# ReLU moved from POOL to ACT and DVE, and state products added in pairs before the fold, in a scan-attention-FFN kernel

## Chip, core and metric

One core of one Trainium2 chip. The metric is the device time of one execution in microseconds (us), lower is better. PE is TensorE, DVE is VectorE, ACT is ScalarE, POOL is GpSimd. The kernel is already tuned: the work of its engines is interleaved by hand, in a fixed program order.

## The reference, cut to what matters

```python
# x: (4, 64, 64, 96); one layer norm without weights is _ln_t
x = x + conv(_gn(x))                    # group norm, then the scan below
t = tokens(x)                           # (4, 4096, 96)
t = t + linear_attention(_ln_t(t))
t = t + ffn(_ln_t(t))

# conv: proj = layernorm(x) @ W_in: value u, gate g, delta d, and A, B, C with 16 states a channel
def step(h, ins):
    A_t, B_t, C_t, d_t, u_t, g_t = ins
    h_new = d * (A_t * h) + d * (B_t * u_t)
    y = g_t * sum(C_t * h_new, axis=states)
# ... then y @ W_out

# ffn: q_mul rounds to fp8 (e5m2), q_acc to fp16
h = relu(q_acc(q_acc(q_mul(x) @ q_mul(W1).T) + q_mul(b1)))      # 384 wide
y = q_acc(q_acc(q_mul(h) @ q_mul(W2).T) + q_mul(b2))
```

## The kernel before

The work is cut into 32 chunks (4 images of 8), each of 512 positions. In a chunk the 96 channels and 16 states make 12 tiles of 128 partitions: 3 channel groups (`NCG`) times 4 state groups (`NSH`). One step of the program handles one tile; everything else is hung into the steps by `at(step, fn)`.

```python
while s < K or any(q >= s for q in steps):
    # ...
    tiles[s + 1].a_proj()          # PE: A of the next tile
    tiles[s].c_proj()              # PE: C of this tile
    last.keep()                    # ACT: last column of the state
    tiles[s + 1].b_mul()           # POOL: bu = bu * du
    last = tiles[s]; last.scan()   # DVE: h = scan(A, bu)
    tiles[s + 1].a_mul()           # DVE: A = (A + bias) * d
    last.c_mul()                   # DVE: ch = (C + bias) * h
    call(s)                        # what hangs in this step
    tiles[s + 2].b_proj()          # PE
    tiles[s + 2].b_copy()          # ACT: bu = B + bias
```

The products `ch` of each state group are folded over states by PE into one bank `y_ps`, four times a chunk, three matmuls each time:

```python
def state_sum(b, i, sh):
    # ...
    for cg in range(NCG):
        nc.tensor.matmul(y_ps[g][cg * 32 : (cg + 1) * 32, :], lhsT=fold,
            rhs=tiles.pop(g * NT + NCG * sh + cg).ch,
            start=(sh == 0), stop=(sh == NSH - 1), ...)
```

The tail of the previous chunk and the FFN of the previous image ride in the same steps. In the tail, `gated` (the multiply yg, on DVE) comes once a chunk and serves below as its clock mark; `ln.apply` makes xa on ACT, `gram` transposes it into a bank of the tag "M", and `keep` copies that to `xat` on ACT. (A bank is a piece of PSUM, the memory that the program's matmuls write to; a tag names one or more banks that are used in turn.) The FFN of a chunk:

```python
def transpose():                   # PE, then ACT: xq
    ps = bank("B" if drain else "M", [C, TC], f"xq_ps_{nm}")
    # ... four transposes
    nc.scalar.activation(v["xq"], ps, AF.Copy, saturate=False)
def hidden(m):                     # PE; the tag "M" has two banks
    v["h", m] = bank(("C", "Y", "M")[m] if drain else "M", [P, TC], f"h_ps{m}_{nm}")
    nc.tensor.matmul(v["h", m], lhsT=w1_q[:, m * P : (m + 1) * P], rhs=v["xq"], ...)
def relu(m):                       # ACT rounds to fp16, POOL adds the bias and cuts at 0
    # ... hq is made at m == 0, one buffer
    nc.scalar.copy(h16, v["h", m])
    nc.gpsimd.tensor_scalar(hr, h16, b1_q[:, m : m + 1], 0.0, ALU.add, ALU.max)
def quant(m):                      # ACT: to fp8
    nc.scalar.activation(v["hq"][:, m, :], v["hr", m], AF.Copy, saturate=False)
```

The last image's FFN (`drain`) has no scan beside it and runs after the last tile.

## Time and profile before

| | before |
|---|---|
| time, median of 3 runs | 1533.5 us (1532.3 to 1540.0) |
| the execution that the trace shows | 1539.95 us |
| chunk of image 0 | 36.1 us, with group norm 37.8 us |
| chunk with FFN (images 1 to 3) | 40.0 to 40.1 us, with group norm 41.0 us |
| from the start of the first scan to the start of the last ("scan stage") | 1288.3 us |
| from the start of the last scan to the end ("drain") | 122.6 us |

A chunk is timed from yg to yg. Five longer chunks, 43.4 to 49.3 us, are left out of the rows: the first chunk of images 1 and 2 and the fifth of images 0 to 2. The drain is timed here from the last scan and not from the last yg, because the change moves yg by one step and leaves the scan where it is. Ahead of the first scan lies a start-up (the group norm of image 0, the preparation of the weights).

The costliest groups of instructions of the profile before name the parts that the change touches. The columns are line, engine, operation, output and inputs, count, then busy us and mean ns of one, then the idle time of the engine ahead of them and what ended it:

```profile
L735 POOL TENSOR_SCALAR hr<-h,b_q 128x512 f16<-128x512 f16 x96 | 191.9, 2000 | 17.2 <-ACT h L733 16.1
L601 PE MATMUL y_ps<-ch,fold 128*32 128x512 f32 x768 | 136.4, 605 | 0.0
L741 ACT ACTIVATE hq<-hr 128x512 fp8e5<-128x512 f16 x96 | 60.5, 630 | 144.6 <-POOL hr L735 139.8
```

The ReLU on POOL takes 2.0 us each, and ACT stood idle 139.8 us over the run until one of them ended. The y sums (folds of the products over the states) count as 136.4 us of PE. These are the two targets.

### The profile page before, as it was taken

What the parts mean: (1) busy time and instruction counts of PE and PEld (TensorE: products, weight loads), DVE (VectorE), ACT (ScalarE), POOL (GpSimd) and SP (SyncE); (2) the same over time, 40 slices, a digit from 0 to 9 for tenths busy, and PEclk for the clock granted to TensorE, in tenths of its full rate; (3) what the DMA queues carried; (4) which work ended last, traced back from release to release, by engine and by line L of the source; (5) the groups of instructions that cost most, each with busy time, mean ns of one, the idle gap of its engine ahead of it and who ended that gap; (6) DMA issues with size and microseconds to landing.
All of it is one profiled execution on the core that took longest, in us unless ns stands there. A gap on an engine that the chain in (4) does not pass through costs nothing.

```text
span 1538.2 us, 20844 instructions
## 1 busy us (share of the span) xinstructions
PE 1374.3 (89%) x6513; PEld 916.4 (60%) x6513; DVE 1201.0 (78%) x2271; ACT 644.8 (42%) x1501; POOL 984.3 (64%) x868
## 2 busy tenths in 40 slices
PE   5847999999999999989999999989999999998652
PEld 4715666666666666656666666566666666665531
DVE  1007999988999988879999898979999999998330
ACT  2013334433333444544444545434445454443343
POOL 4134555546554777767775777777777777666587
PEclk9999999999999999999999999999999999999555
DMA  7002222222222222221222222212222212220001
GB/s 182 20 9 64 59 62 63 62 47 50 51 56 51 59 67 63 54 50 48 55 55 54 62 59 56 56 42 55 56 55 56 55 47 56 55 56 6 11 11 31
DMA packets 82210, 80.98 MB, mean 53 GB/s; under 512 B 49900, under 2 KB 50384, under 8 KB 82099
## 3 DMA queue, kind: packets, MB, share of 16 engines
q1 hardware_dynamic: 80080, 77.22, 21.1%
q10 hardware_dynamic: 2018, 2.43, 0.7%
q8 instruction: 51, 0.84, 0.2%
q14 instruction: 61, 0.49, 0.1%
HBM read 8.72 MB, written 6.29 MB: 10 GB/s over the span
## 4 chain that ended last, share of the span: by engine, by line
PE 41%; POOL 14%; issue 12%; DVE 12%; ACT 8%; SPq 6%; DMA 4%; POOLq 0%; ACTq 0%; DVEq 0%
PE Cps L155 9%; PE Bps L155 8%; PE Aps L155 7%; POOL bu L554 6%; POOL hr L735 5%; SPq L487 5%; PE y_ps L601 4%; DVE h L570 4%; DVE ch L588 3%; PE dug_ps L155 3%; PE a_ps L705 2%; PE o_ps L624 2%; ACT z L305 2%; DMA d<-d 2%; ACT xn L305 2%
## 5 line engine op out<-in xcount | busy, mean ns | idle before, releaser
L554 POOL TENSOR_TENSOR bu<-bu,du 128x512 f32<-128x512 f32 x384 | 493.9, 1286 | 429.9 <-ACT bu L551 243.4
L570 DVE TENSOR_TENSOR_SCAN h<-Aps,state,bu 128x512 f32<-128x512 f32 x336 | 427.8, 1273 | 89.9 <-POOL bu L554 89.0
L551 ACT ACTIVATE bu<-Bps,b_bac 128x512 f32<-128x512 f32 x384 | 262.3, 683 | 414.0 <-PE Bps L155 398.6
L563 DVE SCALAR_TENSOR_TENSOR Aps<-Aps,b_bac,d 128x512 f32<-128x512 f32 x384 | 283.1, 737 | 32.6 <-PE Aps L155 32.0
L155 PE MATMUL Bps<-xs,w 128*128 128x512 f32 x768 | 273.0, 437 | 15.3 <-ACT bu L551 15.3
L588 DVE SCALAR_TENSOR_TENSOR ch<-Cps,b_bac,h 128x512 f32<-128x512 f32 x384 | 284.9, 742 | 0.5 <-PE Cps L155 0.4
L155 PE MATMUL Cps<-xs,w 128*128 128x512 f32 x768 | 252.7, 410 | 10.1 <-DVE ch L588 10.0
L155 PE MATMUL Aps<-xs,w 128*128 128x512 f32 x768 | 245.6, 401 | 7.9 <-DVE h L570 7.8
L735 POOL TENSOR_SCALAR hr<-h,b_q 128x512 f16<-128x512 f16 x96 | 191.9, 2000 | 17.2 <-ACT h L733 16.1
L155 PEld LDWEIGHTS Cps<-xs,w 128*128 128x128 f32 x768 | 136.8, 189 | 73.5 <-DVE ch L588 47.3
L155 PEld LDWEIGHTS Bps<-xs,w 128*128 128x128 f32 x768 | 130.9, 192 | 81.2 <-issue 35.9
L155 PEld LDWEIGHTS Aps<-xs,w 128*128 128x128 f32 x768 | 144.0, 190 | 47.2 <-DVE h L570 14.5
L155 PE MATMUL Bps<-xl,w 128*128 128x512 f32 x384 | 152.9, 398 | 0.0
L155 PE MATMUL Aps<-xl,w 128*128 128x512 f32 x384 | 152.5, 397 | 0.0
L155 PE MATMUL Cps<-xl,w 128*128 128x512 f32 x384 | 152.4, 397 | 0.0
L601 PE MATMUL y_ps<-ch,fold 128*32 128x512 f32 x768 | 136.4, 605 | 0.0
L741 ACT ACTIVATE hq<-hr 128x512 fp8e5<-128x512 f16 x96 | 60.5, 630 | 144.6 <-POOL hr L735 139.8
L305 ACT ACTIVATE xa<-x,nmr_a,rstd_a 128x96 f32<-128x96 f32 x128 | 49.4, 457 | 113.7 <-DVE nmr_a L301 113.7
L155 PEld LDWEIGHTS Bps<-xl,w 128*128 128x128 f32 x384 | 73.1, 190 | 17.4
L155 PEld LDWEIGHTS Aps<-xl,w 128*128 128x128 f32 x384 | 72.7, 189 | 18.1
L305 ACT ACTIVATE z<-z,nmr_c,rstd_c 128x96 f32<-128x96 f32 x128 | 49.4, 457 | 80.6 <-DVE nmr_c L301 80.6
L155 PEld LDWEIGHTS Cps<-xl,w 128*128 128x128 f32 x384 | 72.4, 188 | 17.7
(157 smaller groups left out, 1735.7 us busy)
## 6 DMA issues: line engine op xcount, KB each, us to landing
d<-d SPq DMA_DIRECT2D x384, 64.0 KB, 2.0
du<-du SPq DMA_DIRECT2D x384, 64.0 KB, 2.0
xl<-lo SPq DMA_DIRECT2D x64, 128.0 KB, 2.3
x<-in_x_dram SPq DMA_DIRECT2D x32, 192.0 KB, 2.8
out_dram<-o SPq DMA_DIRECT2D x32, 192.0 KB, 2.3
w<-w SPq DMA_DIRECT2D x18, 128.0 KB, 2.3
xs<-lo SPq DMA_DIRECT2D x32, 64.0 KB, 2.0
raw<-in_L_conv_W_in_dram ACTq DMA_DIRECT2D x3, 576.0 KB, 5.4
```

Source lines behind the costliest of these rows:

```text
L155: nc.tensor.matmul(ps, lhsT=wt[:, n], rhs=mv, start=(n == 0), stop=(n == 2))
L305: nc.scalar.activation(dst[:, j, 0:C], src[:, j, :], AF.Identity, bias=nmr[:, j : j + 1], scale=self.r[:, j : j + 1],)
L487: nc.sync.dma_start(t[q * 32 : (q + 1) * 32, :], src[cg * 32 : (cg + 1) * 32, :])
L551: nc.scalar.activation(self.bu, self.b_ps, AF.Identity, bias=self.bias(0))
L554: nc.gpsimd.tensor_tensor(self.bu, self.bu, rep["du4", self.b, self.i, self.cg], ALU.mult)
L563: nc.vector.scalar_tensor_tensor(self.a_ps, self.a_ps, self.bias(1), rep["d4", self.b, self.i, self.cg], ALU.add, ALU.mult,)
L570: nc.vector.tensor_tensor_scan(self.h, self.a_ps, self.bu, 0.0 if self.i == 0 else state[self.sh, self.cg], ALU.mult, ALU.add,)
L588: nc.vector.scalar_tensor_tensor(self.ch, self.c_ps, self.bias(2), self.h, ALU.add, ALU.mult)
L601: nc.tensor.matmul(y_ps[g][cg * 32 : (cg + 1) * 32, :], lhsT=fold, rhs=tiles.pop(g * NT + NCG * sh + cg).ch, start=(sh == 0), stop=(sh == ...
L624: nc.tensor.matmul(ps[:, j, :], lhsT=yg[:, j * P : (j + 1) * P], rhs=w_o, start=True, stop=True)
L735: nc.gpsimd.tensor_scalar(hr, h16, b1_q[:, m : m + 1], 0.0, ALU.add, ALU.max)
L741: nc.scalar.activation(v["hq"][:, m, :], v["hr", m], AF.Copy, saturate=False)
```

## The change

Intent: take the ReLU off POOL, give POOL the additions of the state groups pairwise (1 onto 0, 3 onto 2), and let PE fold two pairs a chunk in place of four groups. To make the pairs fit, the fold and the tail come a step later, and the FFN is shifted.

```diff
-FFN0 = 15
+FFN0 = 14
...
-            self.ch = work.tile(..., bufs=6)
+            self.ch = work.tile(..., bufs=8)
...
+    def pair_sum(k):
+        t = tiles.pop(k).ch
+        s = tiles[k - NCG].ch
+        nc.gpsimd.tensor_tensor(s, s, t, ALU.add)
...
-            h16 = work.tile([P, TC], F16, tag="h16", name=f"h16_{m}_{nm}")
+            h16 = work.tile([P, TC], F16, tag="h16", name=f"h16_{m}_{nm}", bufs=1)
             nc.scalar.copy(h16, v["h", m])
-            hr = work.tile([P, TC], F16, tag="hr", name=f"hr_{m}_{nm}")
-            nc.gpsimd.tensor_scalar(
-                hr, h16, b1_q[:, m : m + 1], 0.0, ALU.add, ALU.max
-            )
+            hr = work.tile([P, TC], F16, tag="hr", name=f"hr_{m}_{nm}", bufs=1)
+            bias = b1_q[:, m : m + 1]
+            if drain:
+                nc.vector.tensor_scalar(hr, h16, bias, 0.0, ALU.add, ALU.max)
+            else:
+                nc.scalar.activation(hr, h16, AF.Relu, bias=bias)
...
-            at(s0 + 6 + m, hidden, m)
-            at(s0 + 7 + m, relu, m)
+            at(s0 + 7 + m - drain, hidden, m)
+            at(s0 + 8 + m - drain, relu, m)
             at(s0 + 8 + m, quant, m)
...
-            for sh in range(NSH):
-                at(s0 + NCG * (sh + 1), state_sum, b, i, sh)
-            at(s0 + NT, tail, b, i, s0 + NT)
+            for sh in range(0, NSH, 2):
+                for cg in range(NCG):
+                    at(s0 + NCG * (sh + 1) + cg + 1, pair_sum, s0 + NCG * (sh + 1) + cg)
+                at(s0 + NCG * (sh + 2) + 1, state_sum, b, i, sh)
+            at(s0 + NT, tail, b, i, s0 + NT + 1)
```

(`stop` of the fold follows the new last group, the attention matrix moves from step 8 to 9 so that it stays behind the tail, and the loop keeps a set of tiles already made.)

More of the change, by code (lines that the diff above doesn't have):

```diff
@@ L586, in c_mul @@
         def c_mul(self):
-            self.ch = work.tile([P, TC], F32, tag="ch", name=f"ch_{self.nm}", bufs=6)
+            self.ch = work.tile([P, TC], F32, tag="ch", name=f"ch_{self.nm}", bufs=8)
             nc.vector.scalar_tensor_tensor(
@@ L603, in state_sum @@
                 rhs=tiles.pop(g * NT + NCG * sh + cg).ch,
-                start=(sh == 0), stop=(sh == NSH - 1),
+                start=(sh == 0), stop=(sh == NSH - 2),
                 tile_position=(0, 32 * cg), skip_group_check=True,
@@ L693, in attn_matrix @@
         for n, fn in enumerate((gram_out, gk, kv, ff, r)):
-            at(s0 + 8 + n, fn)
+            at(s0 + 9 + n, fn)
     def ffn(b, i, s0, drain):
@@ L811, in conv_attn_hybrid_kernel @@
         s = FRONT
+        made = set()
         while s < K or any(q >= s for q in steps):
             for k in (s, s + 1, s + 2):
-                if 0 <= k < K and k not in tiles:
+                if 0 <= k < K and k not in made:
+                    made.add(k)
                     tiles[k] = Tile(k)
```

## The prediction

> **What bounds the kernel now.** I read the page's head first, then the busy time by stretch, then who waits for whom on VectorE in one period, then the timeline around one wait and the waits of the last stretch. The page:
>
> ```profile
> PE 1374.3 (89%) x6513; PEld 916.4 (60%) x6513; DVE 1201.0 (78%) x2271; ACT 644.8 (42%) x1501; POOL 984.3 (64%) x868
> ```
>
> PE looks like the bound. But the run has three stages. A chunk (512 positions, 12 tiles) can be timed by the start of its gating multiply yg on DVE, which comes once a chunk: about 36.1 to 37.8 us apart in image 0, which has no FFN beside it (the longer ones carry the next image's group norm), 40.1 or 41.0 us in images 1 to 3, and after the last yg at 1418.9 us a drain of 119 us. The busy time in one chunk of image 0, one of image 3, and the drain:
>
> ```profile
> core 0: us, PE busy (x) PEld busy (x) DVE busy (x) ACT busy (x) POOL busy (x), PEclk, DMA share, GB/s
> 437.29:473.53 36.24, 35.96 (x175) 24.96 (x174) 35.00 (x66) 14.30 (x37) 19.64 (x18) 1.00 0.23 53
> 1227.80:1267.90 40.10, 39.21 (x193) 25.93 (x193) 36.45 (x69) 19.61 (x50) 28.50 (x26) 1.00 0.22 53
> 1418.93:1538.00 119.07, 57.76 (x283) 39.75 (x282) 29.45 (x131) 43.98 (x85) 88.10 (x69) 0.53 0.06 17
> ```
>
> Lines 2 and 3: PE is "busy" 98%, but DVE too, 35.0 of 36.2 and 36.45 of 40.1, and DVE's ends are measured. Who DVE waited for in the image 3 chunk:
>
> ```profile
> DVE h L570 <- POOL bu L554: 3.2, 4, 1.0
> DVE Aps L563 <- PE Aps L155: 0.4, 1, 0.4
> ```
>
> 36.45 busy + 3.2 + 0.4 = 40.05 of 40.10. So **DVE and its waits are the whole period**; PE costs DVE 0.4. Its four waits are for bu, POOL's product ahead of each scan. In the timeline two last 0.96 us and follow four row scalings on ACT; two (0.66, 0.67) stand where POOL runs hr. The first kind:
>
> ```profile
> 1248.27 0.20 DVE L301 SCALAR_TENSOR_TENSOR nmr_f<-mv_f,rstd_f 128x4 f32<-128x4 f32 x1
> 1248.48 1.28 DVE L570 TENSOR_TENSOR_SCAN h<-Aps,state,bu 128x512 f32<-128x512 f32 x1
> 1248.50 1.54 ACT L305 ACTIVATE xn<-x,nmr_f,rstd_f 128x96 f32<-128x96 f32 x4 [0.76 <-DVE nmr_f L301]
> ...
> 1249.95 0.67 ACT L551 ACTIVATE bu<-Bps,b_bac 128x512 f32<-128x512 f32 x1
> ...
> 1250.70 1.29 POOL L554 TENSOR_TENSOR bu<-bu,du 128x512 f32<-128x512 f32 x1 [2.25 <-ACT bu L551]
> ...
> 1252.02 1.28 DVE L570 TENSOR_TENSOR_SCAN h<-Aps,state,bu 128x512 f32<-128x512 f32 x1 [0.96 <-POOL bu L554]
> ```
>
> ACT takes its work in order, so the B copy waits behind the four scalings: nmr to xn to copy to bu to scan, 3.54 us from scan to scan. A plain step of DVE (scan, A product, C product) is 1.20 + 0.64 + 0.65 = 2.5 us. Where the step has no other DVE work, the rest is idle.
>
> The drain is another thing: POOL is busy 88 of 119 us, and
>
> ```profile
> ACT hq L741 <- POOL hr L735: 44.2, 25, 3.1
> DVE xn L312 <- POOL rstd_f L279: 33.3, 8, 6.4
> ```
>
> everything waits for POOL. Between 1485 and 1514 us the chunks follow each other every 9.37 us: three hr of 2.0, rstd 1.27, yb and o 0.9 each make 9.1.
>
> **What the Trainium skill says.** "Perfetto Trace Analysis", section "Identifying the Most-Contended Engine", says that matmul occupancy is not a good measure and that occupancy is, for the vector engines. The trace agrees: PE 98% at 40.1 us, DVE's account closes. "GPSIMD Engine Reference", section 3.1, gives 4497 ns for an fp32 add of 2048; a quarter, 1124, is my estimate for 512, and the trace's like-shaped product takes 1286. Its section 4.1 calls one-input work on POOL roughly line-rate; here the one-input hr took 2000 ns, longer than the two-input product: the measurement decides. "SBUF — State Buffer", section "Who interferes with whom", says that DVE blocks against POOL only with two SBUF inputs or in a 2-port mode. Scan and the A and C products read one tensor from PSUM, so more POOL work shouldn't lengthen them; in the drain the four xn, SBUF to SBUF, took 1.05 us with POOL idle and 2.05 beside it, which agrees. "ScalarE: Activation LUTs", section "Table sets", says relu is in every set, so no table load comes, and the built program has the same two loads as before.
>
> **The change, part by part.**
>
> Counts. PE loses two of four y sums per chunk, 0.99 us each: 64 x 0.99 = 63 us of PE, none of it on DVE's account but the 0.4. POOL loses 96 x 2.0 = 192 us of hr and gets 6 x 32 = 192 adds at 1.29 = 247. ACT gets 72 relus; from hq (0.63, same size, no bias pointer) and bu against xq (683 against 590 ns, with and without pointer), 0.72 each, 52 us on an engine half idle. DVE gets 24 relus in the drain, unknown; my estimate 0.35 (the four xn, 384 fp32 in 1.05 us, are four instructions).
>
> Chunk with FFN. Gone: 0.66 + 0.67 behind hr, and 0.4 for A (the y sum before it goes): -1.7. Come: the compiled order shows what the diff hides. The tail moves a step later and the FFN a step earlier relative to it, so xa (not xn) now stands ahead of the plain step, and on ACT the copy xq comes **between xa and the B copy**, and the copy xat **between z and the B copy**. Each adds 0.48 (ACT's spacing) to the 3.54: 4.02 - 2.58 = 1.44 of idle in place of 0.96, twice: +1.0. In the three steps with pair sums and little else POOL needs 2 x 1.28 = 2.56 against DVE's 2.5: +0.1 to 0.2. In the other three it has 3.5 to 3.85 per step against 3.3 to 3.9 on DVE, with a lead of 1.4 us from the step before: 0. PE's y sum waits for the last pair, then runs nearly level with DVE: +0.2. Sum -1.7 + 1.4 = -0.3; over 23 chunks -7.
>
> Chunk of image 0. No hr to remove. Before, its only notable wait was 0.8 behind z: xa fell before a step that also had row statistics. Now xa lies before the plain step: +1.0; z with xat: +0.6; pairs +0.1; A -0.2. About +1.4 for three chunks; for the five with group norm PE cost 2.1 of waits, of which some 1.5 go, but POOL's centring (0.9) now shares a step with a pair: about +1. Together +9.
>
> So I take **the scan stage as unmoved: +2**.
>
> Drain. In its first part two FFN chunks pass as three rounds of copy, hr, hq (3.25 us from hr to hr), now about 1.75 on ACT; the attention matrix's chain lies beside them, so I count 6 us saved by the first drain chunk. Then eight chunks. POOL per chunk falls to 3.1 us. ACT, in its compiled order, with hq, h16 and hr of one buffer each: hq; wait for the y2 matmuls 1.1; hq 0.63; copy 0.5; relu on DVE and its signals 0.5; hq 0.6; copy 0.5; relu 0.5; copy 0.5; xq 0.5; y16 0.5; hq 0.6 make 6.4. DVE's own order puts xn and statistics (2.1 to 3.1) between two relus, about +0.8. So 7.2 in place of 9.37: 8 x 2.15 = -17. Drain -23.
>
> Sum: 1533.5 + 2 - 23 = 1512. The scan terms come from waits that I add on paper, and several would be smaller with a larger lead of POOL or ACT; I put the middle at **1510**.
>
> **Rivals.**
> (a) PE is the bound as its 98% say. Then 2 us go from each of 32 chunks, and with the drain the time is near 1533 - 63 - 23 = 1447. For it: the chain of waits gives PE 41%. Against: DVE's account closes without PE.
> (b) DVE's waits for POOL's hr go and nothing comes in their place: 23 x 1.7 + 23 = 62, so 1471. Against: the compiled ACT order above.
> (c) POOL becomes late in the pair steps: 12 steps in which it has more than before; 1 us more per chunk is 32 us, near 1540. For it: each pair stands ahead of the next product. Against: POOL is 71% busy at most, 28.5 of 40 us now, and gets 1.7 more.
>
> **Range and chances.** The drain gives 15 to 30 us almost surely. The scan stage may be anything from -25 (part of b) to +20 (part of c). So 1488 to 1530 holds it 8 times in 10. The 2% lines are 1502.9 and 1564.2: faster 0.31, same 0.65, slower 0.04.
>
> **What would show it.** In the profile after: drain from the last yg near 96 us, its chunks some 7 us apart, with POOL's share halved. Image 3 chunks near 39.8 us with two waits of about 1.4 us before scans, behind xa with xq and z with xat; none behind hr. Image 0 chunks near 37.5 and 38.7. If those are below 36 and the FFN chunks near 38, then PE was the bound and rival (a) or (b) is right; if DVE waits over 5 us per chunk right behind the pair sums, (c). A DVE relu near 0.7, or held by POOL, would cut the drain's gain by 8 us.

## The result, and the profile after

| | before | after |
|---|---|---|
| median of 4 runs, same rounds | 1535.1 us (1532.3 to 1540.0) | 1511.2 us (1507.5 to 1514.6) |
| ratio, 95% interval | | 0.984 (0.9805 to 0.9876) |

Ratios in this document are the mean time of one kernel's fast runs over the mean of the other's fast runs of the same rounds, so they are not quite the ratio of the medians that stand beside them. The gain of 1.6% is inside the 2% that counts as "same", where the prediction had put it: 1510 us against 1511.2.

The head of the page after, and the group of the pair sums:

```profile
PE 1340.1 (89%) x6129; PEld 923.7 (61%) x6129; DVE 1214.0 (80%) x2295; ACT 698.3 (46%) x1573; POOL 1031.4 (68%) x964
...
L599 POOL TENSOR_TENSOR ch<-ch,ch 128x512 f32<-128x512 f32 x192 | 247.4, 1289 | 0.7 <-DVE ch L588 0.7
```

PE lost 384 instructions but only 34 busy us, and the span lost 25. POOL got 247 us of pair sums for 192 us of ReLU. Where the time went is seen by stretch. After, a chunk of image 0 with group norm (246.03), two without (403.31 and 440.24), two chunks of image 3 (1232.41 and 1313.99) and the drain from its last yg, in the columns of the same view of before (time, busy us of each engine, clock of PE):

```profile
246.03:283.91 37.88, 35.85 (x163) 24.12 (x161) 34.62 (x60) 15.18 (x39) 28.56 (x27) 1.00 0.26 63
403.31:440.24 36.93, 34.38 (x154) 23.89 (x153) 34.45 (x60) 13.30 (x27) 26.89 (x25) 1.00 0.22 51
440.24:478.24 38.00, 36.02 (x167) 26.18 (x166) 35.08 (x65) 14.15 (x36) 26.96 (x25) 0.96 0.22 52
1232.41:1273.17 40.76, 38.69 (x183) 27.07 (x181) 36.98 (x69) 21.89 (x51) 30.01 (x30) 0.96 0.23 54
1313.99:1353.83 39.84, 37.78 (x183) 26.07 (x182) 36.93 (x69) 21.76 (x51) 30.06 (x29) 1.00 0.22 52
1423.11:1512.90 89.79, 55.56 (x283) 37.91 (x282) 33.73 (x155) 44.31 (x85) 31.04 (x40) 0.53 0.08 22
```

The plain FFN chunks come in two kinds, 39.7 to 39.8 us at clock 1.00 and 40.7 to 40.8 at 0.96. Of the 22 FFN chunks from chunk 9 on, 11 have a clock under 1.00; before, 2 had (and these two are among the 11).

The timeline of DVE (start, duration, engine, line, operation; in brackets the idle time ahead and what ended it) gives the last scan of the run, before and then after:

```profile
1415.66 1.28 DVE L570 TENSOR_TENSOR_SCAN h<-Aps,state,bu 128x512 f32<-128x512 f32 x1
```

```profile
1418.50 1.27 DVE L570 TENSOR_TENSOR_SCAN h<-Aps,state,bu 128x512 f32<-128x512 f32 x1
```

So the scan stage ends 2.8 us **later** than before, and the drain from there is 94.4 us (1512.86 - 1418.50) in place of 122.6 (1538.24 - 1415.66), 28.2 less. The first scan, before and after:

```profile
127.34 1.22 DVE L570 TENSOR_TENSOR_SCAN h<-Aps,bu 128x512 f32<-128x512 f32 x1 [8.18 <-POOL bu L554]
```

```profile
125.19 1.22 DVE L570 TENSOR_TENSOR_SCAN h<-Aps,bu 128x512 f32<-128x512 f32 x1 [8.19 <-POOL bu L554]
```

The start-up was thus 2.2 us shorter in the traced execution of after; that this comes with the execution and not with the edit is taken up below, under "Two groups of runs". From first scan to last, the scan stage takes 1293.3 us in place of 1288.3, 5.0 **more**. The whole gain lies in the last tenth of the run; some 1290 us of scan, where most of the changed instructions are, gave nothing. The question is why.

Who DVE waited for in the FFN chunk at full clock (1313.99), columns as before: total us, times, longest:

```profile
DVE h L570 <- POOL bu L554: 2.9, 2, 1.4
```

Two waits of 1.4 us stand in place of four that made 3.2. The timeline around one of them:

```profile
1250.58 1.28 DVE L570 TENSOR_TENSOR_SCAN h<-Aps,state,bu 128x512 f32<-128x512 f32 x1
1250.60 1.54 ACT L305 ACTIVATE xa<-x,nmr_a,rstd_a 128x96 f32<-128x96 f32 x4 [0.76 <-DVE nmr_a L301]
...
1252.05 0.57 ACT L727 ACTIVATE xq<-xq_ps 96x512 fp8e5<-96x512 f32 x1
1252.53 0.67 ACT L551 ACTIVATE bu<-Bps,b_bac 128x512 f32<-128x512 f32 x1
...
1253.27 1.28 POOL L554 TENSOR_TENSOR bu<-bu,du 128x512 f32<-128x512 f32 x1 [2.73 <-ACT state L580]
...
1254.59 1.28 DVE L570 TENSOR_TENSOR_SCAN h<-Aps,state,bu 128x512 f32<-128x512 f32 x1 [1.43 <-POOL bu L554]
```

ACT takes its work in order: in this trace, the order of the program. The FFN's copy xq now stands between the four scalings xa and the copy of B, and the scan that needs that B waits 1.43 us in place of 0.96. The other wait is the same with xat behind z. POOL is named as the releaser, but POOL itself stood idle for 2.73 us ahead of its product.

The extra 1 us of the slow chunks is another thing. The timeline of PE in the chunk from 1232.41:

```profile
1259.37 0.38 PE L731 MATMUL h_ps<-xq,w_q 96*128 96x512 fp8e5 x1 [1.18 <-ACT xat L649]
...
1261.07 1.05 PE L155 MATMUL Aps<-xs,w 128*128 128x512 f32 x2
...
1264.62 0.63 PE L155 MATMUL Aps<-xs,w 128*128 128x512 f32 x2
```

PE stood idle 1.18 us ahead of the first hidden matmul h_ps, until ACT's copy xat released one of the two "M" banks. Soon after, for 3.4 us, the matmuls took nearly twice their time: two of 512 columns 1.05 us in place of 0.63 (last line). In this chunk DVE waited 0.5 us for C and 0.4 for A, which the other chunk has not. Before, no hidden matmul waited for xat, since they had another step. The Trainium skill's page "TensorE: Matmul & The Clock Gate", section "Part 1: The HAM clock gate", describes such a half clock, but after an idle window of about 3.4 us; here 1.2 us were followed by it. The chunk from 1313.99 has the same wait of PE and no slow stretch.

The page calls the window "free-running": it does not start anew with the kernel. The traces show that. In the clock record of each of the twelve traces, all changes of the clock lie on one grid of 3.41 us, which begins 0.7 to 3.1 us after the program's first instruction, at another place in each trace. Every stretch of slow clock in the scan stage of after is one step of the grid. Two pairs of neighbouring steps by stretch (the number before the DMA share is the clock); in the first step of each pair PE has the 1.2 us gap:

```profile
1256.95:1260.36 3.41, 2.03 (x8) 0.95 (x7) 2.90 (x5) 3.05 (x8) 0.68 (x2) 1.00 0.42 98
1260.36:1263.78 3.42, 3.42 (x11) 2.32 (x9) 2.04 (x2) 3.32 (x7) 3.39 (x4) 0.50 0.42 100
...
1338.87:1342.28 3.41, 2.03 (x7) 1.18 (x8) 2.59 (x4) 3.34 (x9) 0.70 (x1) 1.00 0.45 106
1342.28:1345.70 3.42, 3.42 (x16) 2.28 (x15) 2.79 (x4) 3.32 (x7) 3.41 (x4) 1.00 0.40 96
```

PE waited for xat 19 times in the run. Nine gaps were followed by a slow step: they begin 0.98 to 1.56 us after a mark of the grid. Ten were not: they begin 0.74 to 0.93 us after a mark, or 1.68 us and later. So **where the gap falls on the grid** separates them in this trace without exception; in E4 below, with gaps of 1.8 us, it does so in 17 of 19. Why this band of the step and not another is not shown: the first step of both pairs above has the same 2.03 us of busy PE.

Last, DVE itself is busier: 36.93 us a chunk against 36.45. The row-statistics product nmr_f, minimum, median and maximum ns, first and last start:

```profile
L301 DVE SCALAR_TENSOR_TENSOR nmr_f<-mv_f,rstd_f x24: 126/192/1121, 496.5 to 1432.4; 128x4 f32<-128x4 f32 x24
```

```profile
L301 DVE SCALAR_TENSOR_TENSOR nmr_f<-mv_f,rstd_f x24: 144/556/1093, 494.3 to 1428.5; 128x4 f32<-128x4 f32 x24
```

It reads two tiles from SBUF, the memory of the program's work tiles. After, 21 of the 24 end 17 to 25 ns after a product or a sum of POOL ends, whenever they started: in image 3 they start some 0.63 us into a pair sum of 1.29. Without pairs (E2) the median is 187 ns.

### The profile page after: what moved, and what is told of

Same layout as the page of the kernel before. It is cut to its first block, busy times and chain, and to the rows that moved or that the text cites. A ratio compares the mean times of both kernels' runs of the same rounds, so it can differ in the third digit from the quotient of the medians.

```text
span 1512.9 us, 20176 instructions
## 1 busy us (share of the span) xinstructions
PE 1340.1 (89%) x6129; PEld 923.7 (61%) x6129; DVE 1214.0 (80%) x2295; ACT 698.3 (46%) x1573; POOL 1031.4 (68%) x964
## 4 chain that ended last, share of the span: by engine, by line
PE 33%; DVE 16%; POOL 14%; ACT 14%; issue 10%; SPq 5%; DMA 4%; DVEq 0%; POOLq 0%; ACTq 0%
PE Bps L155 8%; POOL bu L554 7%; PE Cps L155 7%; PE Aps L155 6%; DVE h L570 6%; SPq L487 5%; DMA d<-d 3%; DVE ch L588 3%; ACT bu L551 3%; ACT xa L305 3%; PE y_ps L607 2%; POOL ch L599 2%; PE a_ps L711 2%; ACT z L305 2%; PE y_ps L755 1%
## 5 line engine op out<-in xcount | busy, mean ns | idle before, releaser
L155 PE MATMUL Bps<-xs,w 128*128 128x512 f32 x768 | 275.8, 441 | 28.6 <-ACT bu L551 28.2
L155 PE MATMUL Cps<-xs,w 128*128 128x512 f32 x768 | 258.0, 418 | 9.5 <-DVE ch L588 9.1
L599 POOL TENSOR_TENSOR ch<-ch,ch 128x512 f32<-128x512 f32 x192 | 247.4, 1289 | 0.7 <-DVE ch L588 0.7
L607 PE MATMUL y_ps<-ch,fold 128*32 128x512 f32 x384 | 85.0, 616 | 0.9 <-POOL ch L599 0.9
L305 ACT ACTIVATE xn<-x,nmr_f,rstd_f 128x96 f32<-128x96 f32 x96 | 37.0, 456 | 102.3 <-DVE nmr_f L301 102.3
L731 PE MATMUL h_ps<-xq,w_q 96*128 96x512 fp8e5 x96 | 44.0, 459 | 40.9 <-ACT xat L649 19.9
```

The costliest lines, as they stand in the source:

```text
L155: nc.tensor.matmul(ps, lhsT=wt[:, n], rhs=mv, start=(n == 0), stop=(n == 2))
L305: nc.scalar.activation(dst[:, j, 0:C], src[:, j, :], AF.Identity, bias=nmr[:, j : j + 1], scale=self.r[:, j : j + 1],)
L599: nc.gpsimd.tensor_tensor(s, s, t, ALU.add)
```

## The experiments

Ten kernels were run, in three sets; each set shares its runs of the kernel before. (E6, which was E5 with a second hq, did not fit into SBUF and was not run.) The medians of the kernel before were 1533.1 us (E1 to E4), 1536.6 (E5, E7, E8, E9) and 1532.1 (E10, E11). The theory was: the drain's ReLU on DVE is the whole gain; in the scan, moving the ReLU gains, and the pair sums with their shift give it back, through ACT's order. The rivals were PE as the bound, and POOL late behind its pair sums. Diffs of E1 and E3 are against before, of E2 against E1, of E4, E5 and E7 against after, of E8 against E2. Scan and drain are read from the one trace of each kernel, so they leave out the start-up.

| | edit | median, us | ratio to before, 95% | scan + drain, us | FFN chunk, us | slow-clock chunks of 22 |
|---|---|---|---|---|---|---|
| before | | 1535.1 | | 1288.3 + 122.6 | 40.1 | 2 |
| after | | 1511.2 | 0.984 (0.9805-0.9876) | 1293.3 + 94.4 | 39.8 or 40.8 | 11 |
| E1 | ReLU on DVE in the drain alone | 1510.1 | 0.984 (0.9805-0.9877) | 1288.0 + 98.0 | as before | as before |
| E2 | both ReLU moves, no pairs | 1478.6 | 0.963 (0.9594-0.9664) | 1264.8 + 87.4 | 39.2 | 2 |
| E3 | half of the y sums, wrong result | 1522.3 | 0.991 (0.9873-0.9954) | 1277.4 + 122.7 | 40.1 | 2 |
| E4 | after, two copies a step later | 1496.8 | 0.975 (0.9713-0.9786) | 1279.8 + 94.4 | 39.4 or 40.5 | 13 |
| E5 | after, two copies ahead | 1481.2 | 0.965 (0.9613-0.9682) | 1263.7 + 95.4 | 38.9 or 39.9 | 8 |
| E7 | after, scan's ReLU back on POOL | 1708.7 | 1.113 (1.1067-1.1185) | 1477.2 + 105.6 | 48.4 | 22 |
| E8 | E2 with two hq | 1466.9 | 0.956 (0.9525-0.9587) | 1266.0 + 78.1 | 39.2 | 2 |
| E9 | E2, half of the y sums, wrong result | 1449.2 | 0.945 (0.9413-0.9483) | 1239.7 + 87.8 | 38.6 | 3 |
| E10 | E5 with two hq, h16, hr | 1467.3 | 0.956 (0.9529-0.9597) | 1260.3 + 80.6 | 38.9 or 39.9 | 4 |
| E11 | E5 with two hq | 1473.2 | 0.962 (0.9579-0.9658) | 1263.4 + 87.8 | 38.9 or 39.9 | 8 |

### E1: the last image alone

```diff
-            nc.gpsimd.tensor_scalar(
-                hr, h16, b1_q[:, m : m + 1], 0.0, ALU.add, ALU.max
-            )
+            bias = b1_q[:, m : m + 1]
+            if drain:
+                nc.vector.tensor_scalar(hr, h16, bias, 0.0, ALU.add, ALU.max)
+            else:
+                nc.gpsimd.tensor_scalar(hr, h16, bias, 0.0, ALU.add, ALU.max)
```

> The kernel before with one edit: the ReLU of the last image goes to DVE, the other images keep it on POOL; no pair sums, old schedule. In the two traces the stretch from the last gating multiply to the end went from 119.1 to 89.8 us. Theory (all of the gain of the change lies in the drain, the scan stage gives some of it back): about 1535 - 27 = 1508 us, at or a little under the changed kernel's 1511. Rival (the scan stage gained too, by the PE time of the removed y sums): the drain alone is worth less than the whole change, so this stays above 1515.

It measured 1510.07 us, level with the whole change. Its scan chunks are those of before. From its last yg, by stretch:

```profile
1418.46:1513.00 94.54, 57.10 (x283) 40.38 (x282) 32.36 (x155) 43.37 (x85) 40.63 (x45) 0.52 0.08 21
```

94.5 us in place of 119.1: 24 ReLUs on another engine are worth all that the whole change is. POOL is busy 40.6 us there, where it was 88.1.

### E2: the ReLU's moves without the pairs

```diff
             if drain:
                 nc.vector.tensor_scalar(hr, h16, bias, 0.0, ALU.add, ALU.max)
             else:
-                nc.gpsimd.tensor_scalar(hr, h16, bias, 0.0, ALU.add, ALU.max)
+                nc.scalar.activation(hr, h16, AF.Relu, bias=bias)
```

(Shown against E1; four y sums, the schedule and the buffers are those of before.)

> The kernel before with the whole ReLU half of the change (ACT for images 0 to 2, DVE for the last) and none of the pair sums and schedule shifts. Theory (DVE and its waits are the period; the two waits behind hr on POOL, 0.66 + 0.67 us a chunk, go and nothing comes in their place): FFN chunks of image 3 at 38.8 us in place of 40.1, image 0 unmoved at 36.1 and 37.8, drain about 90, so about 1535 - 29 - 23*1.3 = 1476 us. Rival (the relu on ACT, three more in-order operations ahead of a B copy, delays the copy and costs what it saves; or PE bounds): near 1506.

It measured 1478.6 us, 31 less than E1: the ReLU on ACT is worth as much in the scan and the first part of the drain as the DVE ReLU is at the end. A chunk of image 3 by stretch, and who DVE waited for in it:

```profile
1246.60:1285.81 39.21, 38.65 (x194) 26.19 (x193) 36.41 (x69) 21.55 (x52) 22.63 (x22) 1.00 0.23 55
```

```profile
DVE h L570 <- POOL bu L554: 1.9, 2, 1.0
DVE Aps L563 <- PE Aps L155: 0.9, 2, 0.5
```

The two waits behind hr are gone and the two behind the scalings kept their 0.96. With POOL out of the way, PE becomes a part of the account: 0.9 us for A. From first scan to last it takes 23.5 us less than before. So the pairs with what came along with them cost after, against E2, 28.5 us in the scan (1293.3 - 1264.8) and 7.0 in the drain (94.4 - 87.4). The 7.0 are most likely the single buffers of h16 and hr, which the change brings in and E2 has not: E10, with two of each, has a drain 7.2 us shorter than E11 (it also has one bu less).

### E3: is PE the bound in the kernel before? (wrong result)

Only state groups 0 and 2 are folded, so y lacks half of its terms and the output is wrong. PE does as many matmuls as in after, and no other engine gets anything.

```diff
-                start=(sh == 0), stop=(sh == NSH - 1),
+                start=(sh == 0), stop=(sh == NSH - 2),
...
-            for sh in range(NSH):
+            for sh in range(0, NSH, 2):
```

> WRONG RESULT ON PURPOSE: the kernel before with only the y sums of state groups 0 and 2; groups 1 and 3 are computed and dropped. It takes the 64 y sums (63 us of PE) away and adds nothing anywhere. Theory (PE costs DVE 0.4 us a chunk with the FFN, 0.2 or 2.1 us a chunk in image 0): a gain of 23*0.4 + 5*2 = about 20 us at most, so 1515 to 1530. Rival (PE is the bound, as its 98% busy say): 1535 - 63 = 1472.

It measured 1522.3 us. Taking away some 63 us of matmuls by the prediction's count (the busy time of PE fell by 43, from 1374.3 to 1331.5) gained 11, and most of the gain is in image 0 (its chunk with group norm fell from 37.8 to 35.9 us). The FFN chunk by stretch, and its waits:

```profile
1211.01:1251.09 40.08, 38.09 (x181) 25.43 (x181) 36.43 (x69) 19.61 (x50) 28.53 (x26) 1.00 0.23 54
```

It did not move, and DVE's waits in it are, to the digit, the four of before (3.2 us for POOL, 0.4 for PE). PE as the bound of the run, which would be near 1472 here, is ruled out; in the chunks of image 0 with group norm PE did hold DVE up, by the 2 us that went.

### E4: the two copies a step later

```diff
-        at(s0 + 8, keep)
+        at(s0 + 9, keep)
...
-            nc.scalar.activation(v["xq"], ps, AF.Copy, saturate=False)
+        def xq_out():
+            nc.scalar.activation(v["xq"], v["xq_ps"], AF.Copy, saturate=False)
...
         at(s0 + 5, transpose)
+        at(s0 + 6 - drain, xq_out)
```

> The changed kernel with two copies on ACT moved a step later: xq behind the B copy that follows xa, xat behind the B copy that follows z. Nothing else moves. Theory (those two copies lengthen the two waits of the scan from 0.96 to 1.43 us): the waits go back to about 0.96 each, FFN chunks lose 0.9 us and chunks of image 0 lose 0.5, so about 1511 - 25 = 1486. Rival (the period in the changed kernel is set elsewhere, by POOL's pairs or by PE and its clock): within 5 us of 1511.

It measured 1496.8 us, between the 1486 of the theory and the 1511 of its rival. DVE's waits for bu fell to 0.9 us or less, and chunks at full clock to 39.4. But the later xat held the "M" bank longer. Who PE waited for:

```profile
PE h_ps L734 <- ACT xat L649: 1.8, 1, 1.8
```

1.8 us in place of 1.2, and 13 of 22 chunks with a clock below 1.00, the plain ones at 40.5 us. So the theory as first put was half: there is the order on ACT, and there is PE's idle time with the slow clock behind it, and this edit mends the one and worsens the other.

### E5: the two copies ahead

```diff
+    def at_first(step, fn, *args):
+        steps.setdefault(step, []).insert(0, (fn, args))
...
-        at(s0 + 8, keep)
+        at_first(s0 + 8, keep)
...
-        at(s0 + 5, transpose)
+        (at if drain else at_first)(s0 + 5, transpose)
```

The copies now stand ahead of the row scalings on ACT, and the bank comes free earlier.

> The changed kernel with the same two copies on ACT put ahead of the row scalings of their own step instead of a step later: xq (and its transposes on PE) ahead of xa, xat ahead of z. The run with the copies a step later showed scan waits of 0.94, as expected, but TensorE then sat idle 1.8 us (1.2 in the changed kernel) before a hidden matmul that needs the PSUM bank which the xat copy empties, and in the chunks where the granted clock fell to 0.96 VectorE waited 1.2 us for A and C. Theory: here the waits of the scan are 0.94 too, the bank is free early, the idle time and the clock dips go, FFN chunks come to 38.9 us, so about 1475 to 1485. Rival (the bank wait and the clock have nothing to do with it, only the two scan waits count): the same as with the copies a step later, 1497.

It measured 1481.2 us, 30 less than after by an edit of order alone; in the traces the scan stage is 29.6 us shorter (1293.3 - 1263.7). A chunk at full clock:

```profile
1203.70:1242.55 38.85, 36.68 (x183) 25.95 (x181) 36.92 (x69) 21.78 (x51) 30.05 (x30) 1.00 0.24 56
```

DVE's only waits in it are two for bu, 1.9 us together, none longer than 1.0. The wait of PE for xat is gone. The slow clock is not quite: 8 chunks have it, the plain ones at 39.8 to 40.0 us. In six of them the slow stretch follows four transposes (1.39 us together in one of these), ahead of which PE waited 0.7 to 1.0 us for xn; in the other two, the long fifth chunks, it follows a gap of 5 us. Chunks at full clock have the same wait for xn, but elsewhere on the grid: the waits that a slow step follows begin 1.2 to 1.8 us after a mark, the others before 0.7 or after 1.9. The expectation that the slow clock would go held only in part. DVE's 36.92 busy us stay, since nmr_f still meets a pair sum (median 558 ns).

### E7: what if POOL keeps both? (one round)

```diff
             else:
-                nc.scalar.activation(hr, h16, AF.Relu, bias=bias)
+                nc.gpsimd.tensor_scalar(hr, h16, bias, 0.0, ALU.add, ALU.max)
```

> The pair half of the change without the relu half for images 0 to 2: the changed kernel with their ReLU back on POOL (DVE keeps it for the last image). In three steps of each FFN chunk POOL then has 1.28 + 2.0 + 1.28 = 4.56 us for DVE's 2.5. Theory (POOL sets those steps): some 5 us more per FFN chunk than the changed kernel's 40 to 41, so 1511 + 23*5 = about 1625. Rival (POOL has room, 71% busy, and a lead): within 30 us of 1511.

It measured 1708.7 us: the direction of the theory, and a size it had missed by 84 us. The timeline of POOL:

```profile
1407.50 1.28 POOL L599 TENSOR_TENSOR ch<-ch,ch 128x512 f32<-128x512 f32 x1
1408.77 2.00 POOL L745 TENSOR_SCALAR hr<-h,b_q 128x512 f16<-128x512 f16 x1
...
1412.09 1.27 POOL L554 TENSOR_TENSOR bu<-bu,du 128x512 f32<-128x512 f32 x1 [1.32 <-ACT state L580]
```

Pair, ReLU and product make 4.56 us, which I had counted. But in the shifted schedule ReLU and quant of one tile share a step, so ACT's next B copy stands behind hq, which stands behind hr, and POOL idles 1.32 us more: the step is 5.9 us, the chunk 48.4 (at 0.96 of the clock as at 0.89, so the clock, slow in all 22 chunks, is not what sets it). With this schedule the ReLU can't stay on POOL; the two halves of the change belong together in that direction, and only in that one (E2 has the ReLU's move without the pairs, and gains).

### E8 and E9: E2 carried on

E8 gives hq a second buffer:

```diff
-                v["hq"] = work.tile([P, NK, TC], F8, tag="hq", name=f"hq_{nm}", bufs=1)
+                v["hq"] = work.tile([P, NK, TC], F8, tag="hq", name=f"hq_{nm}", bufs=2)
```

> The relu half alone (no pair sums), with a second buffer for hq. In the drain of the changed kernel ACT waits 11.8 us in 7 pieces for the y2 matmuls before it may write the next hq. Theory: 5 to 12 us less than the relu half with one buffer (1478.6), so about 1470. Rival (the drain is then held by PE or DVE at the same pace): unchanged.

It measured 1466.9 us; its time from the last yg is 74.9 us where E2 has 84.1, and ACT's 8.2 us of waits for the matmuls that read the buffer, in E2's drain, are gone.

E9 is E2 with the edit of E3, again a **wrong result**: the ceiling of what the pairs could give if POOL's work were free.

> WRONG RESULT ON PURPOSE: the relu half alone, with the y sums of state groups 0 and 2 only: what pair sums could give at the most, if they cost nothing. The relu half alone has 0.9 us a chunk of waits of DVE for A in the FFN chunks, and dropping half the y sums took 1.9 us from chunks of image 0 with a group norm. Theory: FFN chunks go from 39.2 to about 38.3, so 1478 - 23*0.9 - 12 = about 1446. Rival (DVE's other waits fill the place, as in the kernel before, where FFN chunks did not move at all): 1466.

It measured 1449.2 us, ratio 0.945 against E2's 0.963; its scan stage is 25.1 us shorter than E2's, where E3's was 10.9 shorter than before. So with the ReLU off POOL, PE's y sums are worth some 25 us (28 by the ratios), against 11 with it. The pair sums had something to win; they paid more than that for it.

### E10 and E11: E5 carried on

To make room for the second hq in SBUF, both take one buffer from xat, and E10 one from bu.

```diff
 E10, against E5:
-   bu bufs=4,  xat bufs=NCH + 2,  hq bufs=1,  h16 bufs=1,  hr bufs=1
+   bu bufs=3,  xat bufs=NCH + 1,  hq bufs=2,  h16 bufs=2,  hr bufs=2
 E11, against E5:
-   xat bufs=NCH + 2,  hq bufs=1
+   xat bufs=NCH + 1,  hq bufs=2
```

> Both halves of the change with the two copies ahead, and the drain's buffers as wide as in the relu half alone: two each of hq, h16 and hr, paid for with one bu and one xat buffer less. The last gating multiply stood at 1389.8 us with the copies ahead, a step later in the schedule than in the relu half alone, where it stood at 1395.2; its drain was 90.8 us against 74.9 with the wide buffers. Theory: scan as with the copies ahead, drain near 75 plus 1 to 2, so about 1466 to 1468, level with the relu half alone with two hq (1466.9). Rival (three bu buffers tie the B copy to the scan of a step before): over 1481.

> As the last, but only the second hq, paid for with one xat buffer; bu keeps four, h16 and hr stay at one. Theory (the second hq takes 9 us from the drain, as it did in the relu half alone, and the narrow h16 and hr keep the rest): 1481 - 9 = 1472. Rival (with one h16 and one hr ACT waits for DVE in place of PE, so the second hq gives nothing): 1481.

E10 measured 1467.3 us and E11 1473.2. Set in order and given the same buffers, the version with pairs is level with the one without (E8, 1466.9; the intervals 0.953 to 0.960 and 0.953 to 0.959 lie on each other). Both beat the kernel before by 4.4%.

## Why the prediction was right or wrong

**The time and its split.** 1510 was predicted and 1511.2 measured. The split was +2 in the scan and -23 in the drain; the traces show +5.0 from first scan to last, -28.2 from there on, and -2.2 in the start-up, which has nothing to do with the change. So the scan was missed by 3 and the drain by 5, in opposite directions, and part of the hit is luck. E1 shows the drain's ReLU alone at -23 by the medians, the scan untouched.

**The waits of the FFN chunk: right.** The two waits behind hr went, and two of 1.42 to 1.44 us came where the compiled order put them (1.44 was worked out for both). E4 and E5 show that these waits hang on that order: moved, they fall back to under 1.0. A chunk at full clock is 39.7 to 39.8 us, as predicted, though with other small terms: the 0.1 to 0.2 for POOL in the pair steps and the 0.2 for the fold do not show as waits of DVE, and 0.48 of busy time came, most of it nmr_f. I had quoted the very rule (the Trainium skill's page "SBUF — State Buffer", section "Who interferes with whom": DVE blocks against POOL with two SBUF inputs) and applied it to the three big instructions alone. nmr_f is tiny, has two SBUF inputs, and went from 192 to 556 ns. That relu would bring no table load held: the trace after has two, as before.

**The sum over the FFN chunks: mis-sized.** The term was -7 ("over 23 chunks -7"). From the first scan of image 1 to the last scan of all it measured +1.8 us (986.3 against 984.5). The missing piece is the clock: 9 chunks that ran at full clock before run about 0.9 us longer behind PE's wait for xat, some +8. No step of the prediction looked at which PSUM bank the moved hidden matmul would take and who frees it. Two smaller things were not in it either: FFN chunks with group norm at full clock became 0.1 us longer and not 0.3 shorter (41.08 against 40.96), and the four long chunks of images 1 and 2 became 0.6 to 2.4 us shorter.

**Image 0: mis-sized the other way.** The term was "Together +9". From the first scan of image 0 to that of image 1 it measured +3.2 us (307.0 against 303.8). The chunk with group norm was to become 1 us longer and became 0.1 longer: PE's waits for A of 2.1 us all went, not 1.5 of them, and DVE's waits for POOL rose from 0.9 to 3.2. Chunks without it came to 36.9 and 38.0 around the 37.5 predicted. The two terms were missed by +9 and -6 and so nearly cancelled: that the scan's +2 came near its 5.0 is luck.

**The drain: right in kind, 5 us small.** The DVE ReLU took 0.32 to 0.35 us as estimated, and 0.58 to 0.65 in a few that lay beside POOL; ACT's took 0.72 as estimated. After, by tile:

```profile
L745 ACT ACTIVATE hr<-h,b_q x72: 721/722/726, 507.9 to 1438.4; 128x512 f16<-128x512 f16 x72
L743 DVE TENSOR_SCALAR hr<-h,b_q x24: 320/353/649, 1451.0 to 1504.1; 128x512 f16<-128x512 f16 x24
```

From first ReLU to first ReLU, the eight chunks of the drain followed each other at 6.3, 8.4, 8.0, 8.0, 6.7, 6.4 and 5.6 us, 7.1 in the mean, where 7.2 was predicted. Before, the mean of these seven was 9.0; the prediction's 9.37 held for three of them. The first part of the drain, up to the first of these ReLUs, saved 7.8 us where 6 was counted; the seven steps saved 13.9 and what follows the last first ReLU 6.4, together 20.3 where 17 was counted. Among the largest waits after in the drain are:

```profile
DVE hr L743 <- ACT h L739: 18.1, 10, 3.1
...
ACT hq L749 <- PE y_ps L755: 11.8, 7, 2.8
```

POOL now waits for others (29.2 us in 9 pieces for DVE's statistics mv_f, the longest sum of all), DVE waits for ACT, and ACT waits for PE's second matmuls because hq has one buffer. That a second one is worth 9 us of the drain is shown by E8 (84.1 to 74.9 us from the last yg); with a second h16 and hr as well it is 15 in E10 (76.0 against 90.8 in E5).

**The rivals.** (a), PE as the bound of the run, is dead by E3. (b), the waits of hr go with nothing in their place, did not happen in after, but it is what E2 did: 1478.6 us against the 1471 of (b). (c), POOL late behind the pairs, did not come in the FFN chunks: after, DVE's waits for bu there are fewer and shorter in sum than before (2.9 us against 3.2).

**What the pairs cost** is shown in size (after less E2: 33 us) and for the most part in kind: mending ACT's order (E5) wins back all 28.5 us in the scan (E5's stage is 1263.7 us, E2's 1264.8), and what stays is the drain. So even in order, the pairs gain next to nothing in the scan, though E9 puts 25 us on the matmuls that they save: a chunk at full clock is 0.35 us shorter than E2's (DVE's 0.9 us of waits for A are gone, its busy time is 0.5 longer), but six more chunks have the slow clock, at 1.0 us each. How much of E5's 30 us is DVE's shorter wait and how much the clock, no run tells apart; an estimate from the chunks is 22 us for the wait (22 times the 1.0 by which the two waits fell, from 2.9 to 1.9) and 3 for the clock (three slow chunks fewer); the other 4 lie in image 0 (307.0 against 303.0).

**Two groups of runs.** The runs of the kernel before fall in two groups, about 1532 and 1540 us. The traces point to the start-up. Up to the first scan it takes 127.1 to 127.3 us in before, E1 and E2, 125.2 in after, and 119.4 to 121.5 in the other eight. In these eight the clock record has 6.8 to 10.2 us of full clock within the first 41 us, in after 3.4 us, in the first three none; the same 24 small matmuls (brow_ps) take 5.27 us before and 2.83 in E4. The trace of before is one of the 1540 us group. No trace of a run of 1532 us is kept, so for the kernel before this stays likely and not shown. The ratios use all runs of the same rounds, whichever group they fall in; scan and drain leave the start-up out.

**Open.** Why a gap of PE is followed by the slow clock in one part of the 3.41 us step and not in another.

## What to carry to other kernels

When a change takes work from an engine, find which wait that work stands in, and read from the compiled order of every engine what will stand in its place: here the shift that made room for a new operation put two copies ahead of the one that the critical scan was waiting for, and a change of order alone was worth as much as the change. Try the halves of a change alone, since one half can eat the other's gain. When a matmul moves to another step, ask also which PSUM bank it takes and who frees it, and look at the granted clock of the chunk, not only at the waits. Compare traces stage by stage from a common mark: here a start-up that no edit touched differed by up to 8 us between executions.

## What the Trainium skill lacked or had wrong

- "TensorE: Matmul & The Clock Gate", sections "Part 1: The HAM clock gate" and "HAM oscillation — how this bites in real kernels": the rule is no idle gaps of PE longer than about 3.4 us. Here single gaps of 1.2 us between otherwise dense matmuls (in E5, of 0.7 to 1.0 us with transposes behind them) were followed by 3.4 us of matmuls at nearly twice their time (1.05 in place of 0.63 us), nine times in the changed kernel, for about 0.9 us a chunk. The section that follows there, on psum-queue depth-cycling, does say that frequent short idles of PE can do this; it gives no length. No page says where in the window a short gap counts: here 0.98 to 1.56 us after a mark of the 3.41 us grid.
- "GPSIMD Engine Reference", section 4.1: one-input work is called roughly line-rate and two-input work the slow kind. The one-input fp16 add-and-max of 128x512 took 2000 ns on POOL, and the two-input fp32 add of the same shape 1289 ns.
- "SBUF — State Buffer", section "Who interferes with whom", lacked nothing, and is worth reading for the small instructions: a DVE product of 128x4 with two SBUF inputs went from 192 to 556 ns in the median, because it ended only when POOL's instruction did (21 of 24 ended 17 to 25 ns after it).
